# The MLP's second product in matmuls of 128 moving columns instead of 256

## The chip, the core and the metric

The kernel runs on one core of a Trainium2 chip. The metric is device time in microseconds of one execution. Before the change the median of three runs is 1171.96 us (1169.91 to 1174.85).

## What is computed

Two layers are applied to x, 16 batches of 128 tokens of width 512, all in f32. The first is a decoder layer with 16 heads: self-attention, cross-attention to a context of the same size, and an MLP with a hidden width of 2048. The second is a gated cross-attention to the layer-normalized context. The change lies in the MLP:

```python
x = x + cross_out
ln_out = layernorm(x, ln3_s, ln3_b)
mlp_out = gelu(ln_out @ w1 + b1) @ w2 + b2
return x + mlp_out
```

## The kernel before

**The stages.** The 16 batches are taken in four groups of four (512 tokens each). Section A is self-attention of the four groups, B the cross-attention, then comes the MLP (tile names with C, h, o), and D is the gated attention. Each queue runs in program order: a wrapper (class `InOrder`, line 35) keeps the order in which the code issues instructions, so every row of the profile has line 49, that of the wrapper. Rows are therefore told apart by the names of the tiles.

**The products.** Most of the larger products, the two of the MLP among them, are made by a scheme with seven instead of eight block products. Both operands are cut into halves both ways, certain sums of quarters are formed (on VectorE or GpSimd), seven products of quarters are made, and their sums give the result. A quarter of an operand is a tile of 128 x 2 x 256: 256 rows of the contraction as two chunks k of 128 partitions, and 256 columns.

**The MLP.** `mlp` (line 1032) has 16 steps (line 989): four groups g, and in each four slices i of 512 of the hidden width. In step n the seven products of the first matrix product (`hidden_product`, line 1082, tile h) alternate with the seven of the second product for the step before (`out_product`, line 1132, tile o), in the orders of lines 1175 and 1176, in the loop `for r in range(7)` at line 1227. That makes 16 x 7 = 112 products of each kind. Each is four f32 matmuls: two blocks of 128 rows of the result, times two chunks k that are added up in PSUM. A matmul takes 128x128 weights (of the tokens' side for o: hidden activations h or sums of them, sh) and 256 moving columns (of w2 or sums t of its quarters).

**PSUM.** The h products share one bank (tag mm0). VectorE or ScalarE reads it after each h product, during the o product that follows on TensorE. The seven o products of a group keep a bank each over the four slices (line 1136): the first matmul of the group starts it, the fourth slice ends it, and then `projected_out` (line 1146) adds it into x. An instruction that reads such a bank reads all of it.

**Beside the MLP.** Steps 0 and 1 overlap the last batch of section B, and its out-projections (mo_B) and mixing products (av_B) lie among the h and o products. `beside_mlp` (line 1587) adds loads, layer norms and turned weights for D; four projections of D (mm_q_D) lie between the o products of the last step.

Of the kernel before, what the change touches and what calls it, by code (L numbers as in the profile page):

```python
# [16 lines left out]
P = 128  # L17
# [35 lines left out]
def decoder_then_gated_cross_attention(ctx: ExitStack, tc: tile.TileContext, a: dict, out: bass.AP):  # L53
    nc = InOrder(tc)
# [23 lines left out]
    def afterwards(engine, do):  # L78
        late[engine].append(do)
# [256 lines left out]
    HF = TG // 2  # L336
# [651 lines left out]
    NI = 4  # L988
# [43 lines left out]
    def mlp(ml, last_steps):  # L1032
# [99 lines left out]
        def out_product(n, p, left, right, acc):  # L1132
            g, i = steps[n]
            if i == 0:
                tag, bufs = ("sc", 4) if p < 4 else ("pt", 2) if p < 6 else ("mm1", 1)
                acc[p] = psum.tile([P, 512], F32, tag=tag, name=f"o_{g}_{p}", bufs=bufs)
            for b in range(2):
                for k in range(2):
                    nc.tensor.matmul(
                        acc[p][:, b * HF : (b + 1) * HF], left[:, k, b * P : (b + 1) * P], right[:, k, :],  # L1140
                        start=(i == 0 and b == 0 and k == 0), stop=(i == NI - 1 and k == 1), skip_group_check=True,
                    )
            if i == NI - 1:
                afterwards("dve", lambda: projected_out(g, p, acc[p], acc))

        def projected_out(g, p, mm, acc):
            mm = mm.rearrange("p (b n) -> p b n", n=HF)
            (x11, x12), (x21, x22) = halves(x[g])
            add, gadd = nc.vector.tensor_tensor, nc.gpsimd.tensor_tensor
            if p == 0:  # L1150
                acc["m1"] = quarter(work, "s", f"m1_{g}", 7)
                add(acc["m1"], mm, half_row(ml.b2), ALU.add)
                gadd(x11, x11, acc["m1"], ALU.add)
            elif p == 1:
                add(x11, mm, x11, ALU.add)
            elif p == 3:
                add(x21, x21, mm, ALU.subtract)
            elif p == 5:
                acc["u2"] = quarter(work, "s", f"u2_{g}", 7)
                add(acc["u2"], mm, acc["m1"], ALU.add)  # L1160
                gadd(x12, x12, acc["u2"], ALU.add)
            elif p == 6:
                acc["u3"] = quarter(work, "s", f"u3_{g}", 7)
                add(acc["u3"], mm, acc["u2"], ALU.add)
                gadd(x21, x21, acc["u3"], ALU.add)
                gadd(x22, x22, acc["u3"], ALU.add)
            elif p == 4:
                m5 = quarter(work, "s", f"m5_{g}", 7)
                add(m5, mm, half_row(ml.db2), ALU.add)
                gadd(x12, x12, m5, ALU.add)  # L1170
                gadd(x22, x22, m5, ALU.add)
            elif p == 2:
                add(x12, mm, x12, ALU.add)
# [16 lines left out]
        before, acc = None, {}  # L1190
        for n in range(len(steps) + 1):
# [6 lines left out]
            if n < len(steps):  # L1198
                g, i = steps[n]
# [27 lines left out]
            for r in range(7):  # L1227
                if n < len(steps):
                    p = H_ORDER[r]
                    hidden_product(n, p, sides[p], right1[n][p], h)  # L1230
                if before is not None:
                    p = O_ORDER[r]
                    out_product(n - 1, p, before[0][p], right2[n - 1][p], acc)
                for _ in range(min(2, len(todo))):
                    todo.popleft()()
                for do in at_[r]:
                    if do is not None:
                        do()
                if r == 1 and n + 1 < len(steps):
                    w2[n + 1] = load(n + 1, 2)  # L1240
                elif r == 2 and n + 2 < len(steps):
                    w1[n + 2] = load(n + 2, 1)
                last_steps(n, r)
                if n == 1 and r == 3:
                    for d, t in unkept:
                        nc.sync.dma_start(out=d, in_=t)
                yield
# [428 lines left out]
```

## Time and profile before

| What | Value |
|---|---|
| Median of three runs (lowest to highest) | 1171.96 us (1169.91 to 1174.85) |
| Span of the profiled execution | 1167.4 us, clock granted to TensorE 1.000 |
| Busy TensorE (PE), loads of weights (PEld) | 1129.9 us, 861.9 us |
| Records of matmuls, of weight loads | 7202 each |
| Matmuls into o: 896 records, 128x256 | 379 ns mean of one |
| Weight loads for o: 896 records, 128x128 | 190 ns mean of one |
| o products | from 554.0 to 947 us of the span |

The profiled execution's time outside its span is not listed by itself; the median of the runs is 4.6 us above the span. How to read it: PE is TensorE's matmuls, PEld its weight loads, DVE VectorE, ACT ScalarE, POOL GpSimd, SP the queue that issues DMAs. A row such as "128*128 128x256 f32" is a matmul with 128 rows and 128 columns of weights and 256 moving columns. Each f32 matmul shows as two matmul records, each with a weight load. Matmuls are pipelined: a record's duration (379 ns) is longer than the time from its start to the next one's start. A timeline row with x8 lasts from the first start to the last end of eight records.

### The profile page before, as it was taken

What the parts mean: (1) busy time and instruction counts of PE and PEld (TensorE: products, weight loads), DVE (VectorE), ACT (ScalarE), POOL (GpSimd) and SP (SyncE); (2) the same over time, 40 slices, a digit from 0 to 9 for tenths busy, and PEclk for the clock granted to TensorE, in tenths of its full rate; (3) what the DMA queues carried; (4) which work ended last, traced back from release to release, by engine and by line L of the source; (5) the groups of instructions that cost most, each with busy time, mean ns of one, the idle gap of its engine ahead of it and who ended that gap; (6) DMA issues with size and microseconds to landing.
All of it is one profiled execution on the core that took longest, in us unless ns stands there. A gap on an engine that the chain in (4) does not pass through costs nothing.

```text
span 1167.4 us, 21612 instructions
## 1 busy us (share of the span) xinstructions
PE 1129.9 (97%) x7202; PEld 861.9 (74%) x7202; DVE 760.5 (65%) x1509; ACT 607.5 (52%) x2132; POOL 701.9 (60%) x636
## 2 busy tenths in 40 slices
PE   7999999999999999998999999999999998999998
PEld 5877777657575757545788888888888776778775
DVE  7678878797878777876663633543432249888773
ACT  2567667666766766674221332232222247876663
POOL 7698878688868775684333423533441367564973
PEclk9999999999999999999999999999999999999999
DMA  6587969899888879898796686695457728988864
GB/s 229 149 223 214 251 181 225 247 243 255 203 229 204 244 203 255 246 293 250 268 297 213 197 263 200 191 318 206 154 194 251 199 56 218 253 233 240 251 200 159
DMA packets 325118, 259.75 MB, mean 223 GB/s; under 512 B 83528, under 2 KB 280336, under 8 KB 320144
## 3 DMA queue, kind: packets, MB, share of 16 engines
q1 hardware_dynamic: 324968, 258.38, 77.1%
q8 instruction: 57, 0.93, 0.3%
q14 instruction: 53, 0.43, 0.1%
q10 hardware_dynamic: 40, 0.01, 0.0%
HBM read 163.94 MB, written 94.37 MB: 221 GB/s over the span
## 4 chain that ended last, share of the span: by engine, by line
PE 83%; POOL 5%; DVE 5%; issue 3%; DMA 2%; ACT 1%; SPq 1%; ACTq 0%; DVEq 0%; POOLq 0%
PE o L49 16%; PE h L49 16%; PE mo_A L49 5%; PE mo_B L49 5%; PE mm_q_B L49 4%; PE mm_v_B L49 4%; PE mm_k_B L49 4%; PE mm_k_A L49 4%; PE mm_q_A L49 4%; PE mm_k_D L49 3%; PE mm_v_A L49 3%; PE mm_q_D L49 3%; PE mm_v_D L49 3%; PE sc_B L49 2%; PE av_A L49 1%
## 5 line engine op out<-in xcount | busy, mean ns | idle before, releaser
L49 DVE TENSOR_TENSOR h<-h,h 128x512 f32<-128x512 f32 x80 | 54.9, 686 | 113.6 <-PE h L49 113.6
L49 ACT ACTIVATE s_A<-s_A,mn_A 128x128 f32<-128x128 f32 x256 | 99.5, 393 | 51.2 <-issue 37.3
L49 ACT ACTIVATE h<-h 128x512 f32<-128x512 f32 x64 | 40.3, 630 | 160.6 <-DVE h L49 160.6
L49 ACT ACTIVATE s_B<-s_B,mn_B 128x128 f32<-128x128 f32 x256 | 99.5, 393 | 46.1 <-issue 32.0
L49 ACT ACTIVATE s_D<-s_D,mn_D 128x128 f32<-128x128 f32 x256 | 99.4, 391 | 32.0 <-issue 16.2
L49 POOL TENSOR_TENSOR s_D<-s_D,sum_D 128x512 f32<-128x512 f32 x64 | 66.6, 1041 | 66.3 <-DVE sum_D L49 56.2
L49 POOL TENSOR_TENSOR s_B<-s_B,sum_B 128x512 f32<-128x512 f32 x64 | 66.9, 1046 | 48.9 <-DVE sum_B L49 40.8
L49 POOL TENSOR_TENSOR s_A<-s_A,sum_A 128x512 f32<-128x512 f32 x64 | 66.7, 1041 | 36.0 <-DVE sum_A L49 35.0
L49 POOL TENSOR_TENSOR s_A<-s_A,ma 128x512 f32<-128x512 f32 x64 | 81.9, 1279 | 5.3 <-DVE s_A L49 3.7
L49 POOL TENSOR_TENSOR s_B<-s_B,mask 128x512 f32<-128x512 f32 x64 | 81.4, 1272 | 2.1 <-DMA away_B<-s_B 0.4
L49 POOL TENSOR_TENSOR rstd_aD<-rstd_aD,mhalf 128x1 f32<-128x1 f32 x12 | 6.6, 548 | 114.6 <-DVE rstd_aD L49 101.1
L49 POOL TENSOR_TENSOR sh<-h 128x512 f32<-128x512 f32 x32 | 40.7, 1273 | 51.0 <-ACT h L49 43.0
L49 PE MATMUL h<-T_C,t 128*128 128x256 f32 x256 | 60.7, 380 | 1.4 <-DVE h L49 1.4
L49 PE MATMUL h<-sx,t 128*128 128x256 f32 x256 | 60.7, 380 | 1.3 <-POOL sx L49 1.3
L49 PE MATMUL h<-T_C,w 128*128 128x256 f32 x256 | 61.0, 381 | 0.8 <-DVE h L49 0.8
L49 PE MATMUL mo_B<-w_co,mT_B 128*128 128x512 f32 x128 | 59.0, 604 | 2.4 <-ACT mT_B L49 2.4
L49 PE MATMUL o<-w,h 128*128 128x256 f32 x256 | 60.5, 379 | 0.0
L49 PE MATMUL o<-t,sh 128*128 128x256 f32 x256 | 60.5, 379 | 0.0
L49 PE MATMUL o<-t,h 128*128 128x256 f32 x256 | 60.5, 379 | 0.0
L49 PE MATMUL mo_A<-w_ao,mT_A 128*128 128x512 f32 x128 | 59.1, 605 | 0.0
L49 PE MATMUL mm_q_B<-T_B,w_cq 128*128 128x512 f32 x128 | 57.3, 595 | 0.0
L49 DVE STREAM_TRANSPOSE s_D<-s_D 128x512 f32<-128x512 f32 x60 | 42.3, 705 | 21.4 <-POOL s_D L49 21.2
(324 smaller groups left out, 2996.7 us busy)
## 6 DMA issues: line engine op xcount, KB each, us to landing
t<-kept SPq DMA_DIRECT2D x24, 1024.0 KB, 7.7
away_A<-s_A SPq DMA_DIRECT2D x64, 256.0 KB, 2.9
pT_A<-away_A SPq DMA_DIRECT2D x128, 128.0 KB, 2.9
away_B<-s_B SPq DMA_DIRECT2D x64, 256.0 KB, 4.3
pT_B<-away_B SPq DMA_DIRECT2D x128, 128.0 KB, 3.7
away_D<-s_D SPq DMA_DIRECT2D x60, 256.0 KB, 3.9
pT_D<-away_D SPq DMA_DIRECT2D x120, 128.0 KB, 2.9
w<-in_L_xattn_w_dram SPq DMA_DIRECT2D x24, 512.0 KB, 5.4
```

The source lines that it names most:

```text
L49: return lambda *args, **kw: self.tc.keep_in_program_order(call(*args, **kw))
```

## The change

In `out_product` a loop over two halves n_ of the 256 moving columns is put around the loop over k. Each matmul then has 128 moving columns and writes 128 columns of the result. The weights of a matmul are the same for both halves, but between the two uses lies the other chunk k. The start flag stays on the first matmul of a group's bank alone.

```diff
             for b in range(2):
-                for k in range(2):
-                    nc.tensor.matmul(
-                        acc[p][:, b * HF : (b + 1) * HF], left[:, k, b * P : (b + 1) * P], right[:, k, :],
-                        start=(i == 0 and b == 0 and k == 0), stop=(i == NI - 1 and k == 1), skip_group_check=True,
-                    )
+                for n_ in range(2):
+                    for k in range(2):
+                        nc.tensor.matmul(
+                            acc[p][:, b * HF + n_ * P : b * HF + (n_ + 1) * P], left[:, k, b * P : (b + 1) * P],
+                            right[:, k, n_ * P : (n_ + 1) * P],
+                            start=(i == 0 and b == 0 and n_ == 0 and k == 0), stop=(i == NI - 1 and k == 1),
+                            skip_group_check=True,
+                        )
```

## The prediction

> **What bounds the kernel now.** I began with the page: the busy sums, the slices, and the chain that ended last.
>
> ```profile
> PE 1129.9 (97%) x7202; PEld 861.9 (74%) x7202; DVE 760.5 (65%) x1509; ACT 607.5 (52%) x2132; POOL 701.9 (60%) x636
> ...
> PEclk9999999999999999999999999999999999999999
> ...
> PE 83%; POOL 5%; DVE 5%; issue 3%; DMA 2%; ACT 1%; SPq 1%; ACTq 0%; DVEq 0%; POOLq 0%
> ```
>
> The reader is to see that TensorE holds the chain, at an undiminished granted clock throughout. The same list by line puts the tile o (the products that are changed) at 16% of the span. Then I asked for busy time by stage, here two stretches of 40 us inside the MLP (columns: PE, PEld, DVE, ACT, POOL busy us, clock, DMA share, GB/s):
>
> ```profile
> 680.00:720.00 40.00, 40.00 (x187) 35.23 (x187) 11.57 (x21) 11.84 (x21) 10.47 (x9) 1.00 0.81 246
> ...
> 800.00:840.00 40.00, 40.00 (x187) 35.25 (x186) 13.01 (x23) 7.78 (x15) 14.46 (x13) 1.00 0.60 213
> ```
>
> PE is never idle there, DVE and ACT less than a third of the time busy. From 560 to 960 us PE idles 1.7 us in all. So whatever an o product gains in length is, nearly in full, length of the kernel. Next the timeline at 700 us, matmuls first, then weight loads:
>
> ```profile
> 701.83 1.89 PE L49 MATMUL o<-t,h 128*128 128x256 f32 x8
> 703.56 1.89 PE L49 MATMUL h<-T_C,w 128*128 128x256 f32 x8
> ```
>
> ```profile
> 701.62 1.70 PEld L49 LDWEIGHTS o<-t,h 128*128 128x128 f32 x8
> 703.34 1.70 PEld L49 LDWEIGHTS h<-T_C,w 128*128 128x128 f32 x8
> ```
>
> One product of four f32 matmuls is eight records, each with a weight load of its own: the program has each f32 matmul run as two load-and-matmul pairs. A record lasts 0.379 us (its group's mean), so eight starts span 1.89 - 0.379 = 1.51 us, seven steps of 0.216; the mean over all o records with no wait behind them is 215.85 ns. A product costs 8 x 215.85 = 1.727 us. Each load starts as the matmul before it starts and has 216 ns to finish.
>
> **The change, part by part.** Only PE's instructions differ. In the changed program each of the 112 o products (16 steps of 7) has eight matmuls of 128 columns in place of four of 256; the instructions, order and waits of the other queues, and all else on PE, are the same. So no DMA, tile or wait moves. 112 x 8 = 896 records of 256 columns become 112 x 16 = 1792 of 128, and 896 weight loads become 1792, since the loop over k lies inside the new one and no two neighbours share their weights. The price is the pace of a 128-column record that needs a full 128x128 f32 load. That record does not occur before, so I bound it by its two sides.
>
> The moving side: a record of 512 columns goes every 0.429 us (mo: loads at 1154.91, 1155.34, 1155.77), one of 256 every 0.216: 0.83 ns per column and 3 ns fixed, so 109 to 110 ns at 128. The transposes at the end move 128 columns:
>
> ```profile
> 1149.84 0.60 PE L49 MATMUL tp_D<-ident,s_D 128*128 128x128 f32 x4
> ```
>
> (0.60 - 0.273)/3 = 0.109. But their loads are short (140 ns as recorded, against 190), so they show this side alone.
>
> The loading side: where the wait ended before a load, two loads stand uncovered:
>
> ```profile
> 1154.38 0.30 PEld L49 LDWEIGHTS mo_D<-w_go,mT_D 128*128 128x128 f32 x2 [0.41 <-ACT mT_D L49]
> ```
>
> 0.30 less one load's 0.19 is 0.11: the second starts 108 to 109 ns after the first (over 116 such places the single records give 107 to 110, and the matmul starts 105 to 107 ns after its load). So the recorded 190 ns occupies the array for some 106, and the two sides are about equal. Half of the 216 ns that covered a load today is slack; the change spends all of it. What decides is the handover: a load can begin only when the matmul before it has taken its own weights, some 2 ns after that started, and under a running matmul it is recorded 3 to 4 ns longer (190) than uncovered (186).
>
> Two places show the handover under 128-column matmuls. The scores (32-row weights, four side by side, so 32 records are eight rounds of 128 columns):
>
> ```profile
> 958.22 1.17 PE L49 MATMUL sc_D<-k_D__7898,q_D 32*128 32x128 f32 x32
> ```
>
> 1.17, less the last record's 0.27, the first load's 0.10 and the four starts' spread of 0.02, is 0.78 for seven steps: 0.111. From the single records' starts, four records apart, the mean in the sections A and B is 111.7 ns. The av rounds, with 32-column loads, run mostly at 109; so it is the long load that adds 2.5. The other place is where a full load falls under the last transpose (the eight records after it):
>
> ```profile
> L49 PEld LDWEIGHTS mm_o_D<-gsums_o,sums_mT x8: 190/190/193, 1144.6 to 1146.0; 128*128 128x128 f32 x8
> L49 PE MATMUL mm_o_D<-gsums_o,sums_mT x8: 379/379/382, 1144.7 to 1146.2; 128*128 128x256 f32 x8
> ```
>
> The durations are minimum, median and maximum. By the single records the 382 is the first matmul: it starts 109 ns after the transpose, lasts 3 ns more than the rest, and its successor follows after 219 instead of 216. I read that as a matmul that stood 3 ns waiting for its weights: 109 + 3 = 112. Both places say about 112; I take 111.8.
>
> Sum: 16 x 111.8 = 1.789 us for 1.727, +0.062 per product. One of the 112 (before PE's 1.1 us wait at 572 us, which ends with DVE work) is absorbed: 111 x 0.062 = **+6.9 us**. The lower end is 109: 16 x 109.2 = 1.747, +0.020, +2.3 us. Below that I see no gain: the same columns pass at the same 0.83 ns. The upper end takes the 193 of the second load above as the standing price, 3 ns more than 112: 16 x 115 = 1.840, +12.6 us. I take 111.8 because the long-load row has it as a steady pace, the 193 only once per group.
>
> What stands beside it: DVE empties h's single PSUM bank during the next o product, which grows, so h finds it free as before. DVE's and ACT's waits for PE grow and cost nothing, as PE is never idle for them there. Transfers get more time.
>
> The Trainium skill, page "TensorE: Matmul & The Clock Gate", section "Part 3: Packing small matmuls — row/col tiling", speaks against this change: it says that a weight load overlaps running matmuls only when the row groups differ. The rows above contradict it for full 128-row loads: eight loads and eight matmuls pass in 1.73 us, which leaves no room for 8 x 106 ns of uncovered loading. By that rule a record would cost 106 + 109 = 215 ns, and the sum would be 112 x (16 x 0.215 - 1.727) = +192 us. The page's section "LDWEIGHTS (loading the stationary operand)" gives columns divided by 1.2, an estimate of 107 ns here, which stays hidden under 109 and would make it +2.3 us.
>
> How the base stands: the profiled span is 1167.4 us; the median of the three timed runs, 1171.96, is 4.6 us more, which is taken to lie around the span and to stay. The forecast is a span of 1174.3 and a time of 1171.96 + 6.9 = **1178.9 us**. A measurement of this kernel can tell about 0.5%, 5.9 us, from no change.
>
> **The rivals.**
>
> A, the load stays wholly hidden (the one on the other side, not slower). Place: the 16 records of every o product. The moving columns set the pace, 109.2 ns, and the time is 1171.96 + 2.3 = 1174.3 us. For it: an uncovered load occupies 105 to 107, less than 109. Against it: the 382 and the 111.7. It decides below (1.727 + 5.86/112)/16 = 111.2 ns per record, close to my forecast.
>
> B, the queue can't feed PE. An h and an o product together need 16 + 32 loads and matmuls in 1.73 + 1.79 us: 73 ns for each. Up to 560 us, PE took 3712 + 3713 of them, 75 ns each, and in bursts (32 of the av matmuls and their loads in 1.1 us) far more. So the rate is shown as a mean, but bursts were followed by slow 512-column records. If 75 ns is the feeding limit: 112 x (48 x 0.075 - 3.454) = +16 us, 1188.
>
> C, loads and matmuls serialize: each record about 214 ns, twice the product, +190 us, 1362. Against it: every full-row product of the trace.
>
> D, the change is absorbed elsewhere: PE's later waits for ACT and DVE (0.75 us at 951, 2.5 at 967) shrink. Against it: those engines wait for PE's own results there. At most 3.2 us returns: 1175.7.
>
> That the change doesn't do what it says is excluded by the program's PE queue.
>
> **How the numbers follow.** Forecast (110.8 to 113.5 ns, 1177 to 1182) 0.62; A 0.20; B 0.11; C 0.03; D and other small effects 0.04. The likeliest gives 1178.9. The range runs from A's 1174.0 to the upper bound of the price, 1184.6; it leaves out B and C, 0.14. Slower by over 0.5%: four fifths of the forecast case (0.49), and B and C: 0.63. Within 0.5%: the rest of the forecast (0.13), A and half of the small effects: 0.35. Faster: the other half, 0.02.
>
> **What would show it.** In the timeline of after, an o row of sixteen records should last 15 x 0.112 + 0.273 = 1.95 us (1.91 under A), the h rows still 1.89; o's matmuls should be recorded at 272 to 276 ns, its loads at 190 to 193, with no idle time on PEld in o products; PE's busy time in the MLP stretches stays 40 of 40, and PEclk stays 9. Gaps on PE put down to issue, or a pace that differs between products, would speak for B. It would be wrong if the handover costs nothing, or if a steady stream of long loads has a cost that single ones don't show.

## The result

The changed kernel takes 1178.8 us (median, 1177.59 to 1181.39) against 1172.39 us (1169.91 to 1174.85) before: a ratio of 1.0059, 95% interval 1.0042 to 1.0077. The forecast was 1178.9 us. The ratios given are not the quotients of the medians.

The profile after, first the page, in the lines that answer to those shown of before:

```profile
PE 1137.2 (97%) x8098; PEld 892.0 (76%) x8098; DVE 760.0 (65%) x1509; ACT 607.6 (52%) x2132; POOL 702.1 (60%) x636
...
PEclk9999999999999999999999999999999999999999
```

PE and PEld have 896 records more each (8098 for 7202), the three other engines the same numbers and, within 0.5 us, the same busy times. Next a stretch of the MLP by stage (PE, PEld, DVE, ACT, POOL busy us, clock, DMA share, GB/s):

```profile
680.00:720.00 40.00, 40.00 (x274) 37.63 (x273) 12.31 (x23) 12.38 (x21) 13.32 (x12) 1.00 0.80 239
```

PE is still never idle, at the full clock. Weight loads fill 37.6 of 40 us instead of 35.2. Then the timeline at 700 us, matmuls and, in the second fence, weight loads:

```profile
700.16 1.89 PE L49 MATMUL h<-T_C,t 128*128 128x256 f32 x8
701.89 1.95 PE L49 MATMUL o<-w,sh 128*128 128x128 f32 x16
703.67 1.89 PE L49 MATMUL h<-sx,w 128*128 128x256 f32 x8
```

```profile
700.05 1.60 PEld L49 LDWEIGHTS h<-T_C,t 128*128 128x128 f32 x8
701.67 1.97 PEld L49 LDWEIGHTS o<-w,sh 128*128 128x128 f32 x16
```

From the o product to the h after it, it is 703.67 - 701.89 = 1.78 us; in the prediction's rows of before it was 703.56 - 701.83 = 1.73. The h rows last 1.89 as before. The o row lasts 1.95, its last record 0.275: 15 steps in 1.675 us, 111.7 ns by these rounded numbers. The tile's own view gives the durations (minimum, median, maximum):

```profile
L49 PEld LDWEIGHTS o<-t,h x512: 190/192/192, 563.5 to 954.5; 128*128 128x128 f32 x171
L49 PE MATMUL o<-t,h x512: 272/275/275, 563.8 to 954.7; 128*128 128x128 f32 x171
```

By the single records, 1574 of the 1683 steps from one o record to the next take 111 or 112 ns. The other 109 take 109 or 110: each is the first step of a product that follows another tile. The load of that first record was done under the record before the product, most often one of 256 columns, so it alone passes at the columns' pace. In return the first h record after an o product waits for its load: it is recorded at 382 ns instead of 379, and the next one starts 218 or 219 ns after it instead of 216. The mean step in o is 111.5 ns, and with the wait in h an o product costs some 60 ns more than before (most steps of this growth, from one o product to the next, are 59 to 61 ns).

From the start of the first o record to that of the last the trace has 392.71 us before and 399.12 after: **+6.4 us**. To the end of the last record, which is now a shorter one, it is +6.3. The 112 products at 60 ns would give 6.7; 0.4 us of it are absorbed, where PE had to wait before the change: 0.06 us at 572 us and 0.11 to 0.12 each at three h products, at 655, 752 and 849 us. The first of the three, matmuls and loads, before the change:

```profile
655.11 1.99 PE L49 MATMUL h<-T_C,w 128*128 128x256 f32 x8
655.10 1.59 PEld L49 LDWEIGHTS h<-T_C,w 128*128 128x128 f32 x8 [0.24 <-DVE h L49]
```

And after it:

```profile
658.00 1.89 PE L49 MATMUL h<-T_C,w 128*128 128x256 f32 x8
```

The row is 0.10 us shorter after the change, as its load no longer waits for DVE. The span grew by 8.5 us; where the other 2 us lie is the first experiment.

### The profile page after: what moved, and what is told of

Its sections match the earlier page's. It is cut to its first block, busy times and chain, and to the rows that moved or that the text cites. A ratio compares the mean times of both kernels' runs of the same rounds, so it can differ in the third digit from the quotient of the medians.

```text
span 1175.9 us, 23404 instructions
## 1 busy us (share of the span) xinstructions
PE 1137.2 (97%) x8098; PEld 892.0 (76%) x8098; DVE 760.0 (65%) x1509; ACT 607.6 (52%) x2132; POOL 702.1 (60%) x636
## 4 chain that ended last, share of the span: by engine, by line
PE 52%; DVE 2%; DMA 2%; POOL 2%; ACT 1%; issue 1%; SPq 0%; DVEq 0%; POOLq 0%; ACTq 0%
PE o L49 16%; PE h L49 16%; PE mm_k_D L49 4%; PE mm_o_D L49 3%; PE mm_v_D L49 3%; PE mm_q_D L49 3%; PE mo_B L49 2%; DMA away_B<-s_B 1%; PE av_D L49 1%; PE mo_D L49 1%; PE sc_D L49 1%; PE mm_v_B L49 1%; POOL x L49 1%; DVE s_D L49 0%; ACT s_D L49 0%
## 5 line engine op out<-in xcount | busy, mean ns | idle before, releaser
L49 PEld LDWEIGHTS o<-t,sh 128*128 128x128 f32 x512 | 62.2, 192 | 2.5 <-issue 1.0
L49 PEld LDWEIGHTS o<-t,h 128*128 128x128 f32 x512 | 62.1, 192 | 2.0 <-issue 0.5
L49 PEld LDWEIGHTS o<-w,h 128*128 128x128 f32 x512 | 62.1, 192 | 2.0 <-issue 0.5
L49 PE MATMUL o<-t,h 128*128 128x128 f32 x512 | 62.3, 275 | 0.0
L49 PE MATMUL o<-w,h 128*128 128x128 f32 x512 | 62.3, 275 | 0.0
L49 PE MATMUL o<-t,sh 128*128 128x128 f32 x512 | 62.3, 275 | 0.0
```

The source lines that it names most:

```text
L49: return lambda *args, **kw: self.tc.keep_in_program_order(call(*args, **kw))
```

## The experiments

The theory under test: a 128-column record waits for its 128x128 f32 weight load, which back to back takes 111.5 ns a record; the columns alone would pass in 109. The main rival: the moving side has a dearer fixed part than I took (111.5 = 128 x 0.833 + 4.9), and the load is hidden. Ratios are to the kernel before on the same chip.

**The kernel before again** (no edit).

> The kernel before, unchanged, timed against itself. Every theory: a ratio of 1.000 within about 0.002. It is run for its profile: the span and the granted clock of a second execution of before, and how much lies around the span. If the 2 us by which the changed kernel's span grew outside the MLP (8.5 us in all, 6.2 of them in the MLP) are an accident of one execution, this span differs from 1167.4 us by a similar amount; if they belong to the change, it is 1167.4 within 0.5 us.

Measured: ratio 1.0008 (0.9996 to 1.002), span 1169.9 us where the first profile had 1167.4. From first to last o record it has 392.71 us again, to 0.01 us. The difference lies outside the o products: 0.2 us before the first o record and 2.4 after the last one. The busy time by stage gives TensorE's clock there, 1.00 in the first profile, less here (columns as above):

```profile
520.00:545.00 25.00, 21.88 (x122) 13.47 (x121) 16.82 (x29) 14.55 (x56) 16.80 (x14) 0.86 0.88 254
...
960.00:1000.00 40.00, 35.55 (x279) 28.66 (x282) 35.01 (x67) 30.53 (x117) 27.04 (x25) 0.96 0.77 208
```

The low clock near 527 us thus cost little, since PE reached its first o record only 0.2 us later. In the first profile of the changed kernel 1.3 us lie before the first o record, where no instruction was changed and the clock was 1.00, and 0.9 after the last. So 2 us outside the MLP are no more than one execution differs from another. The own time of this profiled execution is 1171.98, 2.1 us over its span; that of the changed kernel 1177.7, 1.8 over.

**The changed kernel again** (no edit).

> The changed kernel again, beside the others on one chip. Load-handover theory: 128-column records at 111.5 ns, 112 products at 1.784 us for 1.727, so +6.2 us (one product absorbed) and a ratio of 1.0053; a share beyond that, as in the first measurement (1.0059), would be outside the MLP.

Measured: 1.0062 (1.0049 to 1.0076), 1179.62 us. From first to last o record 399.12 us, as in the first profile: +6.4 us, or 1.0055, which both intervals hold. The expected +6.2 was low by 0.1 to 0.2.

**The loop over k outside the halves**, so that neighbouring matmuls share their weights:

```diff
-                for n_ in range(2):
-                    for k in range(2):
+                for k in range(2):
+                    for n_ in range(2):
```

> The changed kernel with the loop over k outside the two halves, so that two neighbouring f32 matmuls have the same weights. Load-handover theory: every record loads its own weights whatever stood there before, 896 x 2 loads, 111.5 ns, the time of the changed kernel (ratio 1.0053 to 1.006 to before). Rival (a load of weights that are already there is skipped or shorter): fewer PEld records, or a pace of 109 and a time of 1174 to 1176 us.

Measured: 1.0052 (1.0035 to 1.0069), 1177.76 us; 8098 loads, pace 111.5, first to last o record 399.12 us. So nothing is skipped or shortened when two neighbouring f32 matmuls load the same tile. Each f32 matmul makes two loads, and what each of the two holds isn't shown, so a load repeated number for number wasn't tried.

**The first product split as well:**

```diff
-                for k in range(2):
-                    nc.tensor.matmul(
-                        mm[:, o * HF : (o + 1) * HF], right[:, k, o * P : (o + 1) * P], left[:, k, :],
...
+                for n_ in range(2):
+                    for k in range(2):
+                        nc.tensor.matmul(
+                            mm[:, o * HF + n_ * P : o * HF + (n_ + 1) * P], right[:, k, o * P : (o + 1) * P],
+                            left[:, k, n_ * P : (n_ + 1) * P], start=(k == 0), stop=(k == 1),
```

> The first product (h) is split in the same way as the second. Load-handover theory: its 112 products also go from 1.727 to 16 x 111.5 = 1.784 us, so +6.2 us more, about 12.5 us over before, ratio 1.0107. Feeding theory (the queue can't deliver a load and a matmul often enough): 64 loads and matmuls in 3.57 us, one per 56 ns, with no slower h product between to catch up; if the limit is the 73 to 75 ns that the trace of before shows as a mean, a pair of products takes 4.7 us, +126 us, and PE shows gaps.

Measured: 1.0124 (1.0108 to 1.014), 1187.3 us. The timeline of its matmuls:

```profile
701.32 1.95 PE L49 MATMUL h<-T_C,t 128*128 128x128 f32 x16
703.11 1.95 PE L49 MATMUL o<-t,sh 128*128 128x128 f32 x16
704.89 1.95 PE L49 MATMUL h<-T_C,t 128*128 128x128 f32 x16
```

h now costs what o costs: 3.57 us from h to h, and 405.31 us from first to last o record, 6.2 more than with o alone. The queue feeds 64 loads and matmuls in 3.57 us, one per 56 ns, without a gap on PE. So feeding is no limit at 73 to 75 ns. The forecast ratio of 1.0107 lies just outside the interval: a miss by some 2 us. This execution reached its first o record at 558.0 us; the other eight profiles did so at 553.9 to 558.2, and of such a delay the seven h products before that record explain at most 0.4 us. What the excess is stays open.

**Four matmuls of 64 columns:** the pair of halves replaced by (0, 64), (64, 128), (128, 192), (192, 256).

```diff
-                for n_ in range(2):
+                for lo, hi in ((0, 64), (64, 128), (128, 192), (192, 256)):
                     for k in range(2):
...
```

> Each 256-column matmul of the second product as four of 64 columns. Load-handover theory: the pace is that of the loads, 108 to 112 ns a record however few columns pass: 32 x 0.108 to 0.112 = 3.46 to 3.58 us a product for 1.727, +192 to +206 us, 1364 to 1379 us. Rival (the moving side with a dearer fixed part, 111.5 = 128 x 0.833 + 4.9): 58 ns a record, 1.86 us a product, +15 us, 1187 us.

Measured: 1.1737 (1.1714 to 1.1761), 1375.48 us. Matmuls, then loads:

```profile
700.54 3.68 PE L49 MATMUL o<-w,sh 128*128 128x64 f32 x32
704.06 1.95 PE L49 MATMUL h<-sx,w 128*128 128x256 f32 x8
```

```profile
700.33 3.76 PEld L49 LDWEIGHTS o<-w,sh 128*128 128x128 f32 x32
```

The 64-column records go at 111 or 112 ns, as the 128-column ones do, and so do the loads: (3.76 - 0.192 - 0.216)/30 = 111.7, the 0.216 being the first load's time under h. Only the first step of a product, whose load was done under h, takes 55 or 56. Half the columns, the same pace: the columns don't set it, and the rival's 1187 us misses by 188.

**160 and 96 columns:**

```diff
-                for n_ in range(2):
+                for lo, hi in ((0, 160), (160, 256)):
                     for k in range(2):
...
```

> Each 256-column matmul of the second product as one of 160 and one of 96 columns. Load-handover theory: 160 columns take 160 x 0.833 + 3 = 136 ns, 96 columns wait for the load and take 111.5: 247.5 ns a pair of records for 215.9, 8 x 0.2475 = 1.980 us a product, +28 us, 1200 us. Rival (fixed part of 4.9 ns on the moving side): 138 + 85 = 223 ns a pair, as with two of 128, so 1178.8 us.

Measured: 1.0243 (1.0226 to 1.0261), 1199.8 us. The timeline names a row by its first record's shape:

```profile
701.51 2.11 PE L49 MATMUL o<-t,sh 128*128 128x160 f32 x16
...
705.22 2.11 PE L49 MATMUL o<-t,sh 128*128 128x160 f32 x16
```

705.22 - 701.51 = 3.71, less h's 1.73, leaves 1.98 us a product, as expected. The 160-column records go at 136 ns, where columns set the pace, the 96-column ones at 111 to 112, where the load does. What one half gains the other can't use. One trap: at the change of shape the recorded starts lie 82 and 165 ns apart; their sum, 247, is 111.5 + 136. I read this as a start that is recorded up to 29 ns before the weights are in, since the duration grows by that much (328 ns instead of 299 for 160 columns, 275 instead of 246 for 96).

**64 weight columns in three of four slices:**

```diff
+                r_ = P if i == 0 else P // 2
...
-                            acc[p][:, b * HF + n_ * P : b * HF + (n_ + 1) * P], left[:, k, b * P : (b + 1) * P],
+                            acc[p][0:r_, b * HF + n_ * P : b * HF + (n_ + 1) * P], left[:, k, b * P : b * P + r_],
```

> The changed kernel, but in three of the four slices the second product loads only 64 of the 128 weight columns, so half of the result's rows lack those slices; only the pace of the records is of interest. Load-handover theory: the load takes some 55 ns and is wholly hidden, so the 128 columns set the pace, 109 ns, in those products, and 111.5 stays in the first slice. Rival (fixed part on the moving side): 111.5 in all. Time: 84 products x 16 x 2.3 ns = 3 us less than the changed kernel, and up to +16 us where PE changes between weights of 128 and 64 columns, if that costs the 93 ns seen between products and the av matmuls: 1176 to 1192 us.

Measured: one time, 1200.76 us, outside the range I gave; the pace as the load theory has it. Matmuls, then loads:

```profile
700.53 1.96 PE L49 MATMUL o<-t,sh 128*64 128x128 f32 x16
702.43 1.99 PE L49 MATMUL h<-T_C,t 128*128 128x256 f32 x8
```

```profile
700.53 1.72 PEld L49 LDWEIGHTS o<-t,sh 128*64 128x64 f32 x16 [0.33 <-issue]
702.42 1.59 PEld L49 LDWEIGHTS h<-T_C,t 128*128 128x128 f32 x8 [0.17 <-issue]
```

With short loads the same 128-column records go at 109 (979 steps) or 110 ns (203), while in the first slice, with full loads, 111.5 remains. An uncovered short load is followed by the next after 55 ns, as expected. So the 2.3 ns over the columns' pace belong to the load; the number of rows of the result, which is halved with it, can't be told apart from it by this run. A limit of 56 ns for each load or matmul, which would also give 111.5 for a pair, is excluded: as many of them pass here in 109. The time is longer because no load is made ahead where the width of the weights changes: it begins with the matmul that uses it (both at 700.53), PEld idles 0.33 and 0.17 us there, and the steps are h to o 309 ns instead of 216, the next 160 instead of 109, o to h 202 instead of 112, the next 320 instead of 216. That is 0.34 us a product; 81 such products (the other three directly follow another o product) give 27 us, less 3 us of pace. First to last o record grew by 24.1 us over the changed kernel. My range held only the first of these steps, twice.

No variant is faster than the kernel before, and none is clearly faster than the changed one. None of the results points to one either: a quarter has 256 columns, so this scheme offers no wider matmul.

## Why the prediction was right

- **TensorE sets the end in the MLP**: right. PE stays busy 40 of 40 us, and the growth of the o products is the only effect of the change that the profiles show; outside them, profiles of one kernel differ by 2.5 us.
- **The price of a product**: forecast 111.8 ns a record, +0.062 us a product; measured 111.5, and +0.060 with the wait that falls to the next h record. The two places it came from, the scores' rounds (111.7) and the one full load under a transpose (109 + 3), were the right rows.
- **What is absorbed**: too small. The prediction took off one product, 0.06 us; four places take off 0.4. It looked for PE's idle time, and a wait of 0.1 us doesn't show there, because the record before it is still running; it shows in h rows of 1.99 us instead of 1.89. This, more than the price, makes +6.3 of the forecast +6.9.
- **Luck**: the time agrees to 0.1 us by luck. The medians differ by 6.4 us, not 6.9, but a fourth execution moved the median of before from 1171.96 to 1172.39. Medians of the same kernel lie more than 1 us apart (1171.31 and 1173.06 in the first experiment).
- **The handover as cause**: that the load and not the columns sets the pace is shown (64 columns, 160 and 96, short loads). What part of 111.5 is the loading and what the handover is not shown: loads in a row go at 111.5 even under 64-column matmuls, an uncovered load is followed by the next after 108. My reading, that a running matmul lengthens the load, wasn't tried apart.
- **Rivals**: A (109 ns) fails, but shows in the first record of a product and where loads are short. The range's lower end, written as A's 1174.0, is 1174.3 by A's own sum; nothing rests on that. B fails: one load or matmul per 56 ns is fed. C fails: nothing serializes, as long as all weights have the same width. D fails: in the first profile after, PE's waits for ACT at the places named are 0.75 and 2.38 us, for 0.75 and 2.48 before.
- **The base**: wrong, without harm. I took 4.6 us to lie around the span; in the timed executions of these kernels it is 1.7 to 3.1. The profiled execution of before was a short one, with no drop of the clock; the forecast of the span, 1174.3, was therefore too low (1175.9). The time didn't suffer, since the 6.9 were added to the median.
- **What would show it**: o rows of 1.95 us, matmuls of 272 to 275 ns and loads of 190 to 192 came as written, and PEclk stayed 9 in every slice. The slices hide that the mean clock fell to 0.998, and in the second profile of the kernel before to 0.994.
- **The Trainium skill's rule** on overlap (page "TensorE: Matmul & The Clock Gate", "Part 3: Packing small matmuls — row/col tiling") doesn't hold for full loads, which pass at 111.5 ns under matmuls. The page's section "LDWEIGHTS (loading the stationary operand)" gives 107 ns as an estimate for 128 columns; an uncovered load agrees (105 to 107), a steady row of them is 111.5.

## What to carry to other kernels

Ask of every matmul row whether columns or weights set its pace: for f32 with 128 weight columns here, it was 0.83 ns per moving column plus some 3 ns, but in a steady row never under 111.5 ns. By these numbers the two cross at about 130 columns, an estimate. Two records of 128 columns in place of one of 256 cost 3% of the product, 160 and 96 cost 15%, four of 64 make it twice as long. When a resource has slack, look for the one place in the trace where that slack is already gone: here the rounds of the scores and one load under a transpose gave the price. And look for short waits in the length of rows as well as in idle time: a wait of 0.1 us was invisible in PE's busy time.

## What the runs showed of the hardware that was not expected

The granted clock drops to 0.5 for 3.4 or 6.8 us at some of PE's longest waits (2.1 to 2.9 us, near 527, 538, 967 and 1126 us in the kernel before, and at the same places of the others). That profile has no such drop before its last work; each of the other eight has one to three. The same work in the second profile of before and, in the second fence, in the first:

```profile
967.43 3.59 PE L49 MATMUL mm_k_D<-gsums_a,gsums 128*128 128x256 f32 x8 [2.48 <-ACT k_D L49]
```

```profile
967.25 1.97 PE L49 MATMUL mm_k_D<-gsums_a,gsums 128*128 128x256 f32 x8 [2.48 <-ACT k_D L49]
```

After the same idle time of 2.48 us the eight records take 3.59 us in the one and 1.97 in the other. In the four timed executions of the changed kernel the mean clock of 0.998, 0.997, 0.995 and 0.994 goes with 1177.7, 1177.6, 1179.9 and 1181.4 us, a difference of more than half of this change. But the clock isn't the whole of what differs: of the 29 executions of the kernel before in the first experiment, those at 0.998 took 1170.0 to 1173.9 us and those at 0.994 took 1171.5 to 1174.7.
